# A float32 5x5 convolution layer, twice: banded 128x128 products against sixteen 32x32 tiles of the TensorE array

## Chip, cores and metric

One core of one Trainium2 chip. The metric is the device time of one execution in microseconds, the median of several runs. Everything is float32: the input, the weights, the products and the result.

## What is computed

Two layers of x = x + conv5x5(groupnorm(x)) on an array of 8 images, 32 channels, 252 x 252. Cut to what matters:

```python
def conv(x, weight):                       # reflect-padded by 2, circular, through the FFT
    xp = jnp.pad(x, ((0, 0), (0, 0), (p, p), (p, p)), mode='reflect')
    wp = jnp.roll(wp, shift=(-k // 2, -k // 2), axis=(-2, -1))      # -3: -5 // 2
    out = ifft2(einsum('bihw,oihw->bohw', fft2(xp), fft2(wp))).real
    return out[:, :, p:-p, p:-p]

def _gn(v, G=16, eps=1e-5):                # 16 groups of 2 channels over the whole image
    g = v.reshape(B_, G, C_ // G, H_, W_)
    m = jnp.mean(g, axis=(2, 3, 4), keepdims=True)
    s = jnp.var(g, axis=(2, 3, 4), keepdims=True)
    return ((g - m) / jnp.sqrt(s + eps)).reshape(v.shape)

x = x + conv(_gn(x), L0_conv_weight)
x = x + conv(_gn(x), L1_conv_weight)
```

Each output value is a sum over 32 input channels and 25 taps. Because of the roll, the rows and columns that a tap reads run from -1 to 254; -1, 252 and 253 are reflections, and 254 wraps to image row or column 2. The statistics of a layer need the whole image, so the second layer of an image can't begin before its first layer has ended.

## The kernel before

The 128 partitions are four quadrants of 32 channels. An image is cut into slots of four rows, one row per quadrant, so that a slot's result fills all 128 partitions of a PSUM tile. An output slot needs the padded rows of two neighbouring slots of the input, `blk` 0 and 1. For each of the 5 column taps there are therefore two products over the whole 128x128 array. Their weights `wt` (built once, lines 84 to 96) are banded: the 32x32 block for input row q and output row r is the tap a = r + 4 - 4 blk - q where that lies in 0 to 4, and zero elsewhere. Of the 2 x 4 x 4 = 32 blocks of a column tap, 4 x 5 = 20 hold weights, so 5/8 of the multiplications count.

An image is 8 chunks of 8 slots (the last has 7). `x` stays in SBUF from load to store, up to two images of it. `finish_stats` (lines 122 to 148) turns the collected moments into mean and 1/std: a VectorE aggregate, a one-column product `pm` that averages over a group's partitions, a few VectorE steps, a second one-column product `pv`, a square root on ScalarE, a Newton step on VectorE. `normalise` (from line 153) writes a chunk of `g`, the normalised, shifted and padded input: four VectorE operations (line 162) and four small ScalarE copies for the padding columns (lines 182 to 185). `conv` (from line 188) takes two slots at a time, 504 columns: 10 products into one PSUM bank (line 201), or 15 where the two slots straddle a chunk and each column range is cut in two halves of 252, then one VectorE addition of the residual into `x` (line 209).

The run (from line 212) goes image by image, layer by layer, chunk by chunk, and normalises one chunk ahead of the products; behind the last chunk of layer 1 the first chunk of the next image is normalised already. The moments for the next image (line 118) are taken during layer 0, those for layer 1 behind each residual addition. Loads and stores are on SyncE's queue; the loads of two images are issued at the start.

## Time and profile before

| what | value |
|---|---|
| median of 2 runs | 4437.72 us (4437.69 to 4437.75) |
| profiled execution, span from first to last instruction | 4439.0 us |
| TensorE (PE) busy | 4296.0 us, 97%, 11424 matmul records |
| weight loads (PEld) busy | 2159.0 us, 49%, as many records |
| VectorE (DVE) busy | 1375.4 us, 31% |
| ScalarE (ACT) busy | 103.1 us, 2% |
| GpSimd (POOL) busy | 7.3 us |
| moved by DMA | 132.59 MB, 30 GB/s over the span |

Times are microseconds from the start of the span, mean times of one instruction are nanoseconds. One float32 product of the program leaves two weight loads and two matmul records, called passes in the following: 5680 products of line 201, 11360 records. The end of a matmul record is modelled by the profiler, so the distance from one start to the next says more than its length. "Idle before" is the time in which the engine waited ahead of a group of instructions, with what ended the wait.

### The profile page before, as it was taken

How to read it: one execution, taken by the hardware profiler on the slowest of the kernel's cores; microseconds unless marked ns; L12 is line 12 of the kernel's file. 1: busy time of each engine (PE TensorE's matmuls, PEld its weight loads, DVE VectorE, ACT ScalarE, POOL GpSimd, SP SyncE). 2: the span in 40 equal slices, each digit the busy share in tenths (PEclk: the TensorE clock that was granted, in tenths of full speed). 3: DMA queues.
4: the chain of work that ended last, by engine and by line, in shares of the span. 5: the costliest groups of instructions: out<-in, count | busy, mean ns of one | idle time of the engine just before them, and what ended most of it. 6: DMA issues, size and time to landing. Idle time of an engine off the chain costs nothing.

```text
span 4439.0 us, 26427 instructions
## 1 busy us (share of the span) xinstructions
PE 4296.0 (97%) x11424; PEld 2159.0 (49%) x11424; DVE 1375.4 (31%) x1726; ACT 103.1 (2%) x609; POOL 7.3 (0%) x27
## 2 busy tenths in 40 slices
PE   4999999999999999999999999999999999999999
PEld 2454445444554445444544454454445544554444
DVE  6423332332333233332333323332322332232321
ACT  0000000000000000000000000000000000000000
POOL 0000000000000000000000000000000000000000
PEclk9999999999999999999999999999999999999999
DMA  9001320023100221002210023100320001100011
GB/s 173 0 0 38 65 44 1 0 47 64 36 0 0 56 55 36 0 0 56 55 36 1 0 56 65 27 0 0 66 55 8 0 10 28 28 9 1 10 28 36
DMA packets 137716, 132.59 MB, mean 30 GB/s; under 512 B 8320, under 2 KB 137344, under 8 KB 137600
## 3 DMA queue, kind: packets, MB, share of 16 engines
q1 hardware_dynamic: 137216, 130.09, 13.9%
q8 instruction: 89, 1.46, 0.1%
q10 hardware_dynamic: 384, 0.82, 0.1%
q14 instruction: 27, 0.22, 0.0%
HBM read 65.85 MB, written 65.03 MB: 29 GB/s over the span
## 4 chain that ended last, share of the span: by engine, by line
PE 97%; DVE 2%; DMA 1%; ACT 0%; issue 0%; SPq 0%; ACTq 0%; DVEq 0%
PE ps L201 96%; DVE g L162 1%; DMA x<-in_x_dram 1%; DVE mv L124 0%; PE pv L135 0%; DVE stats L118 0%; DMA wraw<-in_L_conv_weight_dram 0%; DVE x L209 0%; PE pm L127 0%; DVE dev L130 0%; DVE sq L133 0%; DVE sq L132 0%; ACT g L182 0%; DVE mr L128 0%; SPq L67 0%
## 5 line engine op out<-in xcount | busy, mean ns | idle before, releaser
L201 PE MATMUL ps<-g,wt 128*128 128x504 f32 (+1 forms) x11360 | 4282.6, 539 | 54.4 <-ACT g L185 54.4
L201 PEld LDWEIGHTS ps<-g,wt 128*128 128x128 f32 x11360 | 2147.7, 189 | 2186.5 <-issue 2076.2
L209 DVE TENSOR_TENSOR x<-ps,x 128x504 f32<-128x504 f32 (+1 forms) x512 | 345.1, 674 | 2435.6 <-PE ps L201 2432.5
L162 DVE TENSOR_SCALAR g<-x,mr 32x1764 f32<-32x1764 f32 (+4 forms) x496 | 668.7, 1365 | 578.1 <-PE ps L201 571.8
L118 DVE BATCH_NORM_STATS2 stats<-x 128x6 f32<-128x504 f32 (+1 forms) x512 | 325.2, 669 | 26.6 <-DMA x<-in_x_dram 18.7
L182 ACT COPY g<-g 128x8 f32<-128x8 f32 x128 | 26.2, 205 | 2766.5 <-DVE g L162 2734.5
L127 PE MATMUL pm<-mv,avg 128*128 128x1 f32 x32 | 6.4, 270 | 66.5 <-DVE mv L124 66.5
L127 PEld LDWEIGHTS pm<-mv,avg 128*128 128x128 f32 x32 | 5.3, 207 | 69.6 <-DVE mv L124 69.6
L184 ACT COPY g<-g 128x8 f32<-128x8 f32 x128 | 25.6, 200 | 0.0
L185 ACT COPY g<-g 128x8 f32<-128x8 f32 x128 | 25.6, 200 | 0.0
L183 ACT COPY g<-g 128x8 f32<-128x8 f32 x128 | 25.5, 199 | 0.2
L135 PE MATMUL pv<-sq,avg 128*128 128x1 f32 x32 | 8.0, 318 | 15.2 <-DVE sq L133 15.2
L140 ACT ACTIVATE std<-var 128x1 f32<-128x1 f32 x16 | 3.2, 203 | 800.2 <-DVE var L137 800.2
L181 ACT COPY g<-row 32x252 f32<-32x252 f32 x16 | 6.4, 399 | 432.9 <-PE ps L201 432.9
L124 DVE BATCH_NORM_AGGREGATE mv<-stats 128x2 f32<-128x192 f32 x16 | 15.4, 996 | 0.3
L135 PEld LDWEIGHTS pv<-sq,avg 128*128 128x128 f32 x32 | 6.6, 257 | 16.5 <-DVE sq L133 16.5
L174 ACT COPY g<-g 32x252 f32<-32x252 f32 x16 | 6.4, 401 | 204.2 <-DVE g L162 204.2
L179 ACT COPY g<-g 32x252 f32<-32x252 f32 x16 | 6.4, 401 | 28.3 <-DVE g L162 28.3
L180 ACT COPY g<-g 32x252 f32<-32x252 f32 x16 | 6.4, 400 | 0.2
L176 ACT COPY row<-g 32x252 f32<-32x252 f32 x16 | 6.4, 397 | 0.4
L95 DVE COPY wt<-wraw 32x160 f32<-32x160 f32 x20 | 4.9, 302 | 2.6 <-DMA wraw<-in_L_conv_weight_dram 2.6
L95 POOL COPY wt<-wraw 32x160 f32<-32x160 f32 x20 | 5.5, 315 | 5.5 <-DMA wraw<-in_L_conv_weight_dram 5.3
(21 smaller groups left out, 30.6 us busy)
## 6 DMA issues: line engine op xcount, KB each, us to landing
x<-in_x_dram SPq DMA_DIRECT2D x224, 252.0 KB, 5.2
out_dram<-x SPq DMA_DIRECT2D x224, 252.0 KB, 4.2
x<-in_x_dram SPq DMA_DIRECT2D x32, 220.5 KB, 4.6
out_dram<-x SPq DMA_DIRECT2D x32, 220.5 KB, 3.5
wraw<-in_L_conv_weight_dram ACTq DMA_DIRECT2D x8, 100.0 KB, 5.1
```

The lines of the kernel that those rows point to most:

```text
L95: eng.tensor_copy(t[quads[q], blk, :, (row + 1) % 4, :], wraw[l][quads[q], a, :, :])
L118: nc.vector.bn_stats(stats[b, l][:, (c * CH + j) // 2, :], xt[b, c][:, j : j + n, :].rearrange("p t w -> p (t w)"))
L124: nc.vector.bn_aggr(mv, stats.pop((b, l)).rearrange("p n s -> p (n s)"))
L127: nc.tensor.matmul(pm, avg, mv[:, 0:1], start=True, stop=True)
L135: nc.tensor.matmul(pv, avg, sq, start=True, stop=True)
L162: nc.vector.tensor_scalar(g[rows, dst, 1 : W + 1], src, mr[rows, 0:1], mr[rows, 1:2], ALU.subtract, ALU.mult)
L182: nc.scalar.copy(g[:, :, 0:1], g[:, :, 2:3])
L183: nc.scalar.copy(g[:, :, W + 1 : W + 2], g[:, :, W - 1 : W])
L184: nc.scalar.copy(g[:, :, W + 2 : W + 3], g[:, :, W - 2 : W - 1])
L185: nc.scalar.copy(g[:, :, W + 3 : W + 4], g[:, :, 3:4])
L201: nc.tensor.matmul(ps[:, at : at + m, :], wt[l][:, blk, kc, :], g[:, lo : lo + m, K - 1 - kc : K - 1 - kc + W], start=(i == 0), stop=(i == ...
L209: nc.vector.tensor_add(xs, ps[:, :n, :], xs)
```

## The change

The array is used as 16 tiles of 32x32: tile (g, m) takes its input from quadrant g of the partitions and writes quadrant m of a PSUM bank. All 25 taps of a 32x32 block are products of their own, accumulated in place; no block is zero.

Image layout. In `x0`, the input of layer 0, quadrant q holds rows 63q - 1 to 63q + 65 of the image, 256 columns wide: a row strip with its halo, so some rows are loaded twice. In `x1`, the input of layer 1, quadrant q holds a strip of 63 columns with its halo over all 256 padded rows. A layer takes 8 chunks of 8 rows (the last has 7); a product covers 8 rows x 63 columns, 504 columns, or 441 in the last chunk. The four banks `ps[g]` of a chunk are fed from the four input quadrants, and in each bank the four column tiles m hold the four pieces in the other direction, so that layer 0 turns row strips into column strips and layer 1 turns them back.

`products` issues, per chunk, 25 taps x 4 m x 4 g = 400 products with g innermost. `finish_stats` additionally builds the weights of this image and layer, `wt` = `wraw` / std + `center`, where `center` is the identity at the tap that reads the pixel itself, which is the residual. The mean goes into a bias: a third one-column product `pb` from `wsum`, a quarter of the sum of the raw weights over the taps in each quadrant. No normalised copy is made any more. Evacuation is four ScalarE activations per chunk that add the bias, into `x1` (with VectorE moments behind each) or into a result tile `y` that is stored. `halo`, `halo_rows` and `pad_cols` fill the padding by GpSimd copies. `x0` and `x1` are single buffers: a chunk of the next image is loaded when the products of layer 0 that read it are done. PSUM is one pool of eight banks, shared by the chunks and the small products.

```diff
-    ps_conv = ctx.enter_context(tc.tile_pool(name="ps_conv", bufs=6, space=bass.MemoryType.PSUM))
-    ps_stat = ctx.enter_context(tc.tile_pool(name="ps_stat", bufs=2, space=bass.MemoryType.PSUM))
+    psum = ctx.enter_context(tc.tile_pool(name="psum", bufs=8, space=bass.MemoryType.PSUM))
...
+    x0 = const.tile([P, S + 4, W + 4], F32, tag="x0", name="x0")
+    x1 = const.tile([P, H + 4, S + 4], F32, tag="x1", name="x1")
...
     def finish_stats(b: int, l: int):
...
         nc.vector.tensor_mul(mr[:, 1:2], inv, fix)
-        norm[b, l] = mr
...
+        wt = wpool.tile([P, K * K, C], F32, tag="wt", name=f"wt_{b}_{l}")
+        nc.vector.scalar_tensor_tensor(wt, wraw[l], mr[:, 1:2], center, ALU.mult, ALU.add)
+
+        rm = small.tile([P, 1], F32, tag="rm", name=f"rm_{b}_{l}")
+        nc.vector.scalar_tensor_tensor(rm, mr[:, 0:1], -1.0, mr[:, 1:2], ALU.mult, ALU.mult)
+        pb = psum.tile([P, 512], F32, tag="conv", name=f"pb_{b}_{l}")
+        nc.tensor.matmul(pb[:, 0:1], wsum[l].rearrange("p q o -> p (q o)"), rm, start=True, stop=True)
+        bias = small.tile([P, 1], F32, tag="bias", name=f"bias_{b}_{l}")
+        nc.vector.tensor_copy(bias, pb[:, 0:1])
+        return wt, bias
...
+    def products(b: int, l: int, k: int, wt):
+        n = rows[k]
+        ps = [psum.tile([P, 512], F32, tag="conv", name=f"ps_{b}_{l}_{k}_{g}") for g in range(4)]
+        for a in range(K):
+            for c in range(K):
+                t = a * K + c
+                for m in range(4):
+                    for g in range(4):
+                        if l == 0:
+                            r0, c0 = k * CH + 4 - a, S * m + 4 - c
+                            src = x0
+                        else:
+                            r0, c0 = S * m + k * CH + 4 - a, 4 - c
+                            src = x1
+                        nc.tensor.matmul(
+                            ps[g][quads[m], : n * S],
+                            wt[quads[g], t, :],
+                            src[quads[g], r0 : r0 + n, c0 : c0 + S],
+                            start=(t == 0),
+                            stop=(t == K * K - 1),
+                        )
+        return [p[:, : n * S].rearrange("p (n s) -> p n s", s=S) for p in ps]
+
+    def evac0(b: int, k: int, ps, bias):
...
+        for g in range(4):
+            dst = x1[:, S * g + k * CH + 1 : S * g + k * CH + 1 + n, 1 : S + 1]
+            nc.scalar.activation(dst, ps[g], AF.Identity, bias=bias)
+            nc.vector.bn_stats(st[:, k * 4 + g, :], dst)
...
+    for k in range(NCH + 1):
+        load(0, k)
...
     for b in range(B):
...
+        wt, bias = finish_stats(b, 0)
+        for k in range(NCH):
+            ps = products(b, 0, k, wt)
+            evac0(b, k, ps, bias)
+            halo(k)
+            if b + 1 < B and k:
+                load(b + 1, k - 1)
+        halo_rows()
...
+        wt, bias = finish_stats(b, 1)
+        for k in range(NCH):
+            if b + 1 < B:
+                stats0(b + 1, k)
+                pad_cols(k)
+            ps = products(b, 1, k, wt)
+            evac1(b, k, ps, bias)
```

How the order of TensorE's products moves, at the two places of which the prediction speaks. A name such as `ps_0_0_2_317` is a PSUM tile of layer 0, chunk 0, first slot 2 before the change, and of layer, chunk and input quadrant g after it; the last number is only a serial number. A row stands for one product of the program, or for as many as its "x" says.

The first products of an image on PE, before:

```order
L201 MATMUL ps_0_0_0_302<-g_0_0_280,wt_163 128x504 x10
L201 MATMUL ps_0_0_2_317<-g_0_0_280,wt_163 128x504 x10
L201 MATMUL ps_0_0_4_331<-g_0_0_280,wt_163 128x504 x10
L201 MATMUL ps_0_0_6_345<-g_0_0_280,wt_163 128x504 x5
```

and after:

```order
L190 MATMUL ps_0_0_0_256<-x_70,wt_0_248 32x504
L190 MATMUL ps_0_0_1_257<-x_70,wt_0_248 32x504
L190 MATMUL ps_0_0_2_258<-x_70,wt_0_248 32x504
L190 MATMUL ps_0_0_3_259<-x_70,wt_0_248 32x504
L190 MATMUL ps_0_0_0_256<-x_70,wt_0_248 32x504
L190 MATMUL ps_0_0_1_257<-x_70,wt_0_248 32x504
L190 MATMUL ps_0_0_2_258<-x_70,wt_0_248 32x504
L190 MATMUL ps_0_0_3_259<-x_70,wt_0_248 32x504
```

Before, ten products in a row fill one bank. After, each product names another input quadrant than the one ahead of it, and the same tile of the array comes back after 16 products, with the next tap.

Between layer 0 and layer 1 of an image on PE, before:

```order
L201 MATMUL ps_0_7_6_829<-g_0_7_713,wt_163 128x252 x10
L127 MATMUL pm_1_845<-mv_1_842,avg 128x1
L135 MATMUL pv_1_853<-sq_1_850,avg 128x1
L127 MATMUL pm_0_1380<-mv_0_1377,avg 128x1
L135 MATMUL pv_0_1388<-sq_0_1385,avg 128x1
L201 MATMUL ps_1_0_0_886<-g_1_0_866,wt_185 128x504 x10
```

and after, here and then between layer 1 of an image and layer 0 of the next:

```order
L190 MATMUL ps_0_7_3_3239<-x_70,wt_0_248 32x441
L142 MATMUL pm_1_3679<-mv_1_3676,avg 128x1
L150 MATMUL pv_1_3687<-sq_1_3684,avg 128x1
L170 MATMUL pb_1_3704<-rm_1_3702,wsum_83 128x1
L190 MATMUL ps_1_0_0_3717<-x_71,wt_1_3700 32x504
```

```order
L190 MATMUL ps_1_7_3_6667<-x_71,wt_1_3700 32x441
L142 MATMUL pm_0_7084<-mv_0_7081,avg 128x1
L150 MATMUL pv_0_7092<-sq_0_7089,avg 128x1
L170 MATMUL pb_0_7109<-rm_0_7107,wsum_77 128x1
L190 MATMUL ps_0_0_0_7113<-x_70,wt_0_7105 32x504
```

Before, the small products of the next image's layer 0 stand between layers 0 and 1 of this one, and nothing of the kind stands between images. After, `pm`, `pv` and `pb` stand ahead of the first product of each of the 16 layers.

## The prediction, made before the changed kernel had run

> **What bounds the kernel now.** I read the page's totals and its chain first, then the groups of line 201 with their shapes kept apart, then the timeline of weight loads in a quiet stretch.

> ```profile
> span 4439.0 us, 26427 instructions
> PE 4296.0 (97%) x11424; PEld 2159.0 (49%) x11424; DVE 1375.4 (31%) x1726; ACT 103.1 (2%) x609; POOL 7.3 (0%) x27
> PE 97%; DVE 2%; DMA 1%; ACT 0%; issue 0%; SPq 0%; ACTq 0%; DVEq 0%
> ```

> The chain that ended last runs through PE for 97%. What PE does there, and at which pace:

> ```profile
> L201 PE MATMUL ps<-g,wt 128*128 128x504 f32 x8800 | 3757.9, 586 | 54.4 <-ACT g L185 54.4
> L201 PE MATMUL ps<-g,wt 128*128 128x252 f32 x2560 | 564.9, 375 | 0.0
> L209 DVE TENSOR_TENSOR x<-ps,x 128x504 f32<-128x504 f32 x496 | 338.4, 682 | 2384.3 <-PE ps L201 2381.2
> L118 DVE BATCH_NORM_STATS2 stats<-x 128x6 f32<-128x504 f32 x496 | 319.2, 677 | 26.3 <-DMA x<-in_x_dram 18.7
> ```

> ```profile
> 1000.09 0.19 PEld L201 LDWEIGHTS ps<-g,wt 128*128 128x128 f32 x1 [0.23 <-issue]
> 1000.51 0.19 PEld L201 LDWEIGHTS ps<-g,wt 128*128 128x128 f32 x1 [0.23 <-issue]
> ...
> 1005.59 0.19 PEld L201 LDWEIGHTS ps<-g,wt 128*128 128x128 f32 x1 [0.24 <-issue]
> ```

> The mean of 586 ns is no price, since records overlap. The price is the distance of starts: 13 passes in 5.50 us, 0.423 us for a pass of 504 columns. A pass of 252 is taken at half, 0.2115. So 8800 x 0.423 + 2560 x 0.2115 = 4264 us, 96% of the span: the kernel is bound by columns streamed through the array. Weight loads fit into the shadow of the passes (0.19 of each 0.42 us), and VectorE waits for PE.

> **What the change removes.** Before, 158,760 columns per image and layer went through the whole array (63 slots x 252 x 10 products). After, each of 16 tiles has 25 taps x 63 x 63 = 99,225 columns, 5/8 of that. In passes: 8 images x 2 layers x 8 chunks x 400 = 51,200 products, 102,400 passes, 89,600 of 504 columns and 12,800 of 441 (0.370 us in proportion). If all 16 tiles stream side by side at the pace above: (89,600 x 0.423 + 12,800 x 0.370) / 16 = 2665 us.

> **What it adds: nine times as many loads and passes.** No row shows a 32x32 tile. The nearest rows are one-column products, where the load alone sets the pace:

> ```profile
> 879.18 0.19 PEld L135 LDWEIGHTS pv<-sq,avg 128*128 128x128 f32 x1 [1.19 <-DVE sq L133]
> ...
> 879.29 0.19 PEld L135 LDWEIGHTS pv<-sq,avg 128*128 128x128 f32 x1
> 879.39 0.19 PEld L127 LDWEIGHTS pm<-mv,avg 128*128 128x128 f32 x1
> ```

> ```profile
> 879.42 0.25 PE L127 MATMUL pm<-mv,avg 128*128 128x1 f32 x1
> ```

> Three loads start 0.105 us apart with a one-column pass between: that is a load of 128 columns plus a pass of nothing. A tile's load has 32 columns. If the time goes with columns, a load and its pass cost 0.026 us, and 102,400 of them, one at a time, 2688 us. If nothing shrinks, 0.105 us and 10,750 us. If loads into different tiles overlap, less than 2688, and the 2665 of the columns is the bound. I take 2688: the row is a load of the same engine and type, and I see no fixed part in it that I could separate. The two bounds lie within 1% of each other, so there is no slack: a fifth more per load gives 3226.

> The rest of the sum are stretches in which PE stands still. Today's, between layers 0 and 1 of image 1:

> ```profile
> 874.65 1.01 PE L201 MATMUL ps<-g,wt 128*128 128x252 f32 x4
> 877.69 0.38 PE L127 MATMUL pm<-mv,avg 128*128 128x1 f32 x2 [2.02 <-DVE mv L124]
> ...
> 881.32 0.15 DVE L147 TENSOR_TENSOR mr<-inv,fix 128x1 f32<-128x1 f32 x1
> ...
> 886.97 5.43 PE L201 MATMUL ps<-g,wt 128*128 128x504 f32 x8 [5.76 <-ACT g L185]
> ...
> 889.65 0.34 PEld L201 LDWEIGHTS ps<-g,wt 128*128 128x128 f32 x1 [0.50 <-issue]
> 890.49 0.25 PEld L201 LDWEIGHTS ps<-g,wt 128*128 128x128 f32 x1 [0.50 <-issue]
> 890.97 0.19 PEld L201 LDWEIGHTS ps<-g,wt 128*128 128x128 f32 x1 [0.24 <-issue]
> ```

> It is 11.3 us, 5.5 of them for normalising. From `pm` to 1/std takes 3.8 (877.69 to 881.47). Behind it the first four passes go at 0.84 instead of 0.42 us, at half the clock: 1.7 us lost. For the new operations I use

> ```profile
> L182 ACT COPY g<-g 128x8 f32<-128x8 f32 x128 | 26.2, 205 | 2766.5 <-DVE g L162 2734.5
> L174 ACT COPY g<-g 32x252 f32<-32x252 f32 x16 | 6.4, 401 | 204.2 <-DVE g L162 204.2
> L124 DVE BATCH_NORM_AGGREGATE mv<-stats 128x2 f32<-128x192 f32 x16 | 15.4, 996 | 0.3
> L95 POOL COPY wt<-wraw 32x160 f32<-32x160 f32 x20 | 5.5, 315 | 5.5 <-DMA wraw<-in_L_conv_weight_dram 5.3
> ```

> ScalarE: 0.196 us for 244 columns more, so 0.6 us for an evacuation of 504 and 0.55 for one of 441. VectorE: 682 ns for 504 elements with two inputs, so 1.1 us for the 800 weights.

> Layer 0 to layer 1, eight times: last evacuations 4 x 0.55 = 2.2, last moments 0.6, aggregate 1.0, `pm` to 1/std 3.8, weights 1.1, `pb` behind them 0.6 = 9.3 us, 74 in all. GpSimd's ten `halo` and four `halo_rows` copies at about 0.3 (4.2 us) start with the last evacuation and end under the VectorE chain; without that cover they would cost 4. Layer 1 to the next image's layer 0, seven times: today nothing, since the next image is normalised ahead. After, `pm`, `pv` and `pb` stand in PE's order behind the last product of the image, so 3.8 + 1.1 + 0.6 = 5.5 us lie open, 38 in all. Behind each of the 15 gaps 1.7 us for the half clock: 25.

> ```profile
> 53.71 1.33 DVE L162 TENSOR_SCALAR g<-x,mr 64x2016 f32<-64x2016 f32 x1
> ```

> ```profile
> 4432.54 2.61 SPq L72 DMA_DIRECT2D out_dram<-x  x4
> ```

> Head: the statistics of the first image are ready at 53.7 us; weights and `pb` add 1.7 and the extra halo rows under one: 56. Tail: today 6.5 us from the last store's issue to the end, plus four evacuations: 9.

> At nothing I cost the folded normalisation, the addition and the padding, as PE covers them: 768 moments x 0.68 = 520 us of VectorE, 512 evacuations x 0.6 = 310 of ScalarE, some 930 small GpSimd copies x 0.3 = 280, all spread under 2700 us. The loads of the next image wait for layer 0's products of the same rows and have all of layer 1 to land.

> **Sum:** 2688 + 56 + 74 + 38 + 25 + 9 = 2890 us, against the 4439.0 of the profiled execution, which lies 1.3 above the median; 2890 stands for both. What surrounds the products is 202 us. The break-even follows: 4439 - 202 = 4237 us for the products, which is 0.0414 us per pass, or 10.1 tiles busy on average out of 16.

> [...] No run here shows tiles yet; the forecast rests on passes that follow each other without draining, as the rows of 1000 us show for the whole array.

> **Rivals.** (a) *The two passes of one product stand in each other's way.* Every product is load, pass, load, pass on the same tile. In the rows at 1000 us the pace is that of one pass at a time. If TensorE starts passes strictly in order, the second pass waits 0.423 us for the first, everything behind it waits too, and only the second pass of one product and the first of the next overlap. Two tiles are busy: 2665 x 8 + 202 = 21,500 us. It decides as soon as fewer than 10.1 tiles stay busy. For it: the in-order pace of today's passes. Against it: they all use the whole array, so no row shows whether a free tile may start past a busy one. [...]

> (b) *A load and a pass have a price that doesn't shrink.* In the rows at 879 us a pass starts 0.03 us after its load (879.39, 879.42). If that is the time to issue an instruction and loads (0.026) and passes take turns, a pair costs some 0.052 us: 102,400 x 0.052 + 202 = 5530 us. It decides above 0.0414. For it: nothing in the trace hides instructions this small. Against it: a part of the 0.03 may be the load's own.

> (c) *Faster, but held back.* Fewer than 16 tiles busy on average, because tiles drain before they start anew (13 tiles give 3480 us, 10.3 give 4340), or PE waiting for its instructions:

> ```profile
> q8 instruction: 89, 1.46, 0.1%
> x<-in_x_dram SPq DMA_DIRECT2D x224, 252.0 KB, 5.2
> ```

> 22,848 loads and passes were fetched in 89 packets, so 204,800 need about 800, one every 3.4 us where it was one every 50. If each refill cost 5.2 us, as a transfer of `x` does from issue to landing, and nothing ran ahead, that is 4160 + 202 = 4360, hardly a gain; if they are read ahead, nothing. Between them, 3450 to 4350.

> **How the numbers follow.** Forecast: 0.48, own range 2840 (2665 for the products, gaps a little smaller) to 3450 (a fifth more per load, 3226 + 202). (c) 0.15. Within 2%, which is about what a measurement can tell from no change: 0.03. (b) 0.14, up to 6000. (a) 0.20. Faster 0.63, same 0.03, slower 0.34. From 2840 to 6000 lie 0.80; only (a) is left out.

> **What would show it.** Right: start to start of passes near 0.026 us, different tiles started before one has ended, PE's share of the chain above 90%, eight gaps of 9 us and seven of 5. (a) would show passes 0.42 us apart in pairs; (b) an even pace above 0.04 whatever the columns, so that the last chunks with 441 columns take as long as the others; (c) PE idle for "issue" at a regular distance of 256 instructions. The size of the gaps is wrong if `halo_rows` ends after the weights.

## The result

The changed kernel takes 3475.15 us (median of 2 runs, 3473.38 to 3476.93) against 4437.72 before: ratio 0.7831, 95% interval 0.7808 to 0.7853, so 22% faster. The forecast was faster, 2890 us. The direction and the surroundings of the products came out as worked out; the products themselves took 585 us more than the 2688 and the 25 for slow starts together.

The page of the kernel after, and two of its groups with shapes kept apart:

```profile
span 3475.2 us, 209222 instructions
PE 3305.6 (95%) x102496; PEld 2632.3 (76%) x102496; DVE 375.8 (11%) x755; ACT 307.6 (9%) x529; POOL 206.8 (6%) x971
...
q8 instruction: 802, 13.14, 1.6%
...
PE 90%; issue 6%; DVE 2%; DMA 1%; ACT 1%; ACTq 0%; DVEq 0%
```

```profile
L190 PE MATMUL ps<-x,wt 32*32 32x504 f32 x89600 | 2907.3, 601 | 14.3 <-issue 13.7
L190 PEld LDWEIGHTS ps<-x,wt 32*32 32x32 f32 x102400 | 2612.0, 103 | 682.4 <-issue 176.7
L190 PE MATMUL ps<-x,wt 32*32 32x441 f32 x12800 | 392.1, 542 | 8.5 <-issue 8.5
```

TensorE still carries the chain. The counts are those foretold, 89,600 and 12,800 passes, and 802 packets of instructions for the 800. The 95% of PE says nothing about full tiles, because a record of 601 ns counts as busy whether one tile or sixteen are at work. The distance of starts says it. The windows view of PE in an undisturbed stretch (length, busy time, passes in it, clock, share of DMA, GB/s):

```profile
1600.00:1700.00 100.00, 99.76 (x3154) 1.00 0.19 45
```

A pass every 0.0317 us, so 1.015 us for the 32 passes of 16 products, where the columns of 16 tiles take 0.846. Below I call these 16 products, one per tile, a turn. From the first to the last start of a layer's passes, summed over the 16 layers of the trace, the products take 3298 us; divided by 3200 turns that is 1.031, slow starts and the shorter turns of the last chunks included.

The rest of the span is 177 us: 52.9 ahead of the first product, eight gaps of 9.6 to 9.9 between layers 0 and 1, seven of 5.1 to 5.6 between images, 8.4 behind the last start. One gap of the first kind, from the timeline (start, length, engine):

```profile
258.48 3.33 PE L190 MATMUL ps<-x,wt 32*32 32x441 f32 x87
...
261.78 2.19 ACT L204 ACTIVATE x<-ps,bias 128x441 f32<-128x441 f32 x4 [23.19 <-PE ps L190]
...
264.66 1.02 DVE L139 BATCH_NORM_AGGREGATE mv<-stats 128x2 f32<-128x192 f32 x1
...
265.83 0.54 PE L142 MATMUL pm<-mv,avg 128*128 128x1 f32 x2 [4.02 <-DVE mv L139]
...
266.84 0.45 POOL L224 COPY x<-x 128x67 f32<-128x67 f32 x2
...
269.32 1.05 DVE L165 SCALAR_TENSOR_TENSOR wt<-wraw,mr,center 128x800 f32<-128x800 f32 x1
...
270.59 0.56 PE L170 MATMUL pb<-rm,wsum 128*128 128x1 f32 x2 [2.72 <-DVE rm L168]
271.08 0.28 PEld L190 LDWEIGHTS ps<-x,wt 32*32 32x32 f32 x32
```

Evacuations, moments, aggregate, `pm` to weights to `pb` follow each other as listed in the forecast, and the `halo_rows` copies (266.84) are done well before the weights.

The start of the first layer, same view, holds the key to the missing 585 us:

```profile
52.85 0.27 PEld L190 LDWEIGHTS ps<-x,wt 32*32 32x32 f32 x32
52.85 4.03 PE L190 MATMUL ps<-x,wt 32*32 32x504 f32 x64
...
53.69 0.17 PEld L190 LDWEIGHTS ps<-x,wt 32*32 32x32 f32 x1 [0.57 <-issue]
54.53 0.64 PEld L190 LDWEIGHTS ps<-x,wt 32*32 32x32 f32 x31 [0.67 <-issue]
55.37 0.17 PEld L190 LDWEIGHTS ps<-x,wt 32*32 32x32 f32 x1 [0.20 <-issue]
```

After a gap a pass takes 0.84 us, twice the 0.42 of the stream. Behind the next gap, where the starts have the same steps, the windows view (same columns) gives a granted clock of one half:

```profile
271.10:275.90 4.80, 4.80 (x93) 0.50 0.02 5
```

### The profile page after: what moved, and what is told of

The parts are those of the page before. It is cut to its first block, busy times and chain, and to the rows that moved or that the text cites. A ratio compares the mean times of both kernels' runs of the same rounds, so it can differ in the third digit from the quotient of the medians.

```text
span 3475.2 us, 209222 instructions
## 1 busy us (share of the span) xinstructions
PE 3305.6 (95%) x102496; PEld 2632.3 (76%) x102496; DVE 375.8 (11%) x755; ACT 307.6 (9%) x529; POOL 206.8 (6%) x971
## 3 DMA queue, kind: packets, MB, share of 16 engines
q8 instruction: 802, 13.14, 1.6%
## 4 chain that ended last, share of the span: by engine, by line
PE 90%; issue 6%; DVE 2%; DMA 1%; ACT 1%; ACTq 0%; DVEq 0%
PE ps L190 89%; DMA x<-in_x_dram 1%; ACT y L230 1%; DVE stats L205 1%; DVE wt L165 0%; DVE mv L139 0%; PE pb L170 0%; DMA wraw<-in_L_conv_weight_dram 0%; PE pv L150 0%; ACT x L204 0%; PE pm L142 0%; DVE fix L160 0%; DVE inv L157 0%; DVE mr L162 0%; DVE stats L135 0%
## 5 line engine op out<-in xcount | busy, mean ns | idle before, releaser
L190 PE MATMUL ps<-x,wt 32*32 32x504 f32 x102400 | 3284.0, 594 | 22.9 <-issue 22.2
L190 PEld LDWEIGHTS ps<-x,wt 32*32 32x32 f32 x102400 | 2612.0, 103 | 682.4 <-issue 176.7
L204 ACT ACTIVATE x<-ps,bias 128x504 f32<-128x504 f32 (+1 forms) x256 | 152.1, 679 | 1555.0 <-PE ps L190 1555.0
L230 ACT ACTIVATE y<-ps,bias 128x504 f32<-128x504 f32 (+1 forms) x256 | 151.8, 677 | 1525.4 <-issue 1233.8
L205 DVE BATCH_NORM_STATS2 stats<-x 128x6 f32<-128x504 f32 (+1 forms) x256 | 154.1, 665 | 1208.0 <-ACT x L204 1208.0
L215 POOL COPY x<-x 32x96 f32<-32x96 f32 x192 | 52.4, 273 | 2800.5 <-ACT x L204 2795.2
L135 DVE BATCH_NORM_STATS2 stats<-x 128x6 f32<-128x504 f32 (+1 forms) x256 | 154.0, 664 | 226.3 <-DMA x<-in_x_dram 226.2
L92 POOL COPY x<-x 128x8 f32<-128x8 f32 (+1 forms) x288 | 43.9, 201 | 232.9 <-DMA x<-in_x_dram 228.8
L170 PE MATMUL pb<-rm,wsum 128*128 128x1 f32 x32 | 8.7, 342 | 44.1 <-DVE rm L168 44.1
L216 POOL COPY x<-x 32x32 f32<-32x32 f32 x192 | 45.1, 235 | 8.6
L165 DVE SCALAR_TENSOR_TENSOR wt<-wraw,mr,center 128x800 f32<-128x800 f32 x16 | 16.8, 1052 | 0.6
L218 POOL COPY x<-x 32x32 f32<-32x32 f32 x64 | 15.4, 240 | 2.6
L219 POOL COPY x<-x 32x32 f32<-32x32 f32 x64 | 15.3, 239 | 0.0
L220 POOL COPY x<-x 32x32 f32<-32x32 f32 x64 | 15.1, 236 | 2.6
L217 POOL COPY x<-x 32x32 f32<-32x32 f32 x64 | 14.8, 232 | 2.7
## 6 DMA issues: line engine op xcount, KB each, us to landing
x<-in_x_dram SPq DMA_DIRECT2D x248, 252.0 KB, 4.9
out_dram<-y SPq DMA_DIRECT2D x224, 252.0 KB, 4.0
x<-in_x_dram SPq DMA_DIRECT2D x32, 31.5 KB, 2.7
```

The costliest lines, as they stand in the source:

```text
L92: nc.gpsimd.tensor_copy(x0[:, r, d : d + 1], x0[:, r, s : s + 1])
L135: nc.vector.bn_stats(st[:, (k * CH + i) // 2, :], x0[:, a : a + n, 1 : W + 1])
L165: nc.vector.scalar_tensor_tensor(wt, wraw[l], mr[:, 1:2], center, ALU.mult, ALU.add)
L170: nc.tensor.matmul(pb[:, 0:1], wsum[l].rearrange("p q o -> p (q o)"), rm, start=True, stop=True)
L190: nc.tensor.matmul(ps[g][quads[m], : n * S], wt[quads[g], t, :], src[quads[g], r0 : r0 + n, c0 : c0 + S], start=(t == 0), stop=(t == K * K ...
L204: nc.scalar.activation(dst, ps[g], AF.Identity, bias=bias)
```

## The experiments

The rivals of A: B, every load and pass has a fixed price of 0.0315 us; C, a tile's pass streams more slowly than one of the whole array; F, PE is paced by the fetching of its instructions. Times of single runs stand beside runs of the kernel before on the same chip, 4439 to 4441 us.

### Another order of the tiles

```diff
-                for m in range(4):
-                    for g in range(4):
+                for g in range(4):
+                    for m in range(4):
```

> Same products, but m innermost: four products in a row now share the input quadrant (row group) and differ in the column tile. The trace after shows 16 products taking 1.006 us on average where the columns alone would take 0.846, and 177 us around the products. Theory A (instructions are held only some 16 products ahead, so that a tile stands empty for 0.16 us between its products), theory B (every load and pass costs 0.0315 us, whatever its columns) and theory C (a pass of a tile streams more slowly than one of the whole array, 0.503 us for 504 columns) all expect the time after, 3475 within 1%. [...]

Measured: 3471.21 us, ratio to before 0.7818 (0.7805 to 0.7831); the interval overlaps that of the kernel after. Whether neighbouring products share an input quadrant makes no difference here.

### Unbroken rows of input

```diff
+                        flat = src.rearrange("p r w -> p (r w)")
...
-                            src[quads[g], r0 : r0 + n, c0 : c0 + S],
+                            flat[quads[g], r0 * src.shape[2] + c0 : r0 * src.shape[2] + c0 + n * S],
```

> Each product reads 504 (441) neighbouring columns in one run where it reads 8 (7) runs of 63: other data, so the output is not the reference's; all counts stay. Theory A and theory B: 3475, unchanged. Theory C, if the short runs are what slows a pass: 16 products in 0.846 us, 3200 x 0.846 + 71 of slow starts + 177 = about 2950.

Measured: 3461.56 us, one run, 14 less than the kernel after. So the short runs of 63 cost at most about that. C falls as far as it blamed them.

### Eight tiles in two quadrants

```diff
-        ps = [psum.tile(...) for g in range(4)]
+        ps = [psum.tile(...) for g in range(2)]
...
-                    for g in range(4):
+                    for g in range(2):
...
-        return [... for p in ps]
+        return [... for p in ps + ps]
```

> Half of the products are left out: only input quadrants 0 and 1, so 8 tiles; banks 2 and 3 are replaced by 0 and 1 in the evacuation. Theory A: 16 products held ahead are now two turns of each tile, so no tile waits, 8 products in 0.846 us, about 2950. Theory B: 8 products cost 0.503, less than the 0.846 that the columns take, so again about 2950. Theory C with a cause in each pass: 8 products in 1.006 us, 3475, unchanged; C with a shared limit (reads or writes of 16 streams): down towards 2950.

Measured: 5472.66 us, which no expectation had: half of the products, and longer than the kernel before. The groups and the timeline of that run:

```profile
L190 PE MATMUL ps<-x,wt 32*32 32x504 f32 x44800 | 4708.0, 1041 | 0.0
L190 PEld LDWEIGHTS ps<-x,wt 32*32 32x32 f32 x51200 | 1423.9, 171 | 3848.4 <-issue 3848.2
```

```profile
1600.08 0.22 PEld L190 LDWEIGHTS ps<-x,wt 32*32 32x32 f32 x8 [0.62 <-issue]
1600.92 0.22 PEld L190 LDWEIGHTS ps<-x,wt 32*32 32x32 f32 x8 [0.62 <-issue]
1601.76 0.22 PEld L190 LDWEIGHTS ps<-x,wt 32*32 32x32 f32 x8 [0.62 <-issue]
```

Four products every 0.84 us, so eight in 1.68: that is two passes of 0.84, the length that a pass has at half clock (the records are 1041 ns long, as in the first microseconds after a gap, 52.85 to 53.89). The weight loads are longer too, 0.17 us as at 53.69 above against 0.10 in the kernel after. The whole run went at the pace of the half clock. The clock column of the windows view shows 1.00 for it, but the trace of this run holds no clock event at all, where that of the kernel after holds 32, so the column says nothing here. At that pace the eight tiles run without any loss between their products, 1.68 of 1.68. So a tile does not stand empty as such. But the hand-over, 0.17 us, is short beside passes of 0.84, and the test of A had to be made again at full clock, below.

### Half the columns

```diff
-                            ps[g][quads[m], : n * S],
+                            ps[g][quads[m], : (n if t == 0 else n // 2) * S],
...
-                            src[quads[g], r0 : r0 + n, c0 : c0 + S],
+                            src[quads[g], r0 : r0 + (n if t == 0 else n // 2), c0 : c0 + S],
```

> 24 of the 25 taps cover only the first half of the columns (252 of 504): work left out, all counts stay. Theory A: 0.423 + 0.16 = 0.583 us for 16 products, about 2170. Theory B: unchanged, 3475. Theory C: in proportion, 0.503, about 1920.

Measured: 3291.38 us, between B (3475) and A (2170), near B. The weight loads in the timeline show that neither number describes it:

```profile
1600.06 1.45 PEld L190 LDWEIGHTS ps<-x,wt 32*32 32x32 f32 x60
1602.52 2.26 PEld L190 LDWEIGHTS ps<-x,wt 32*32 32x32 f32 x128 [1.01 <-issue]
1606.82 0.24 PEld L190 LDWEIGHTS ps<-x,wt 32*32 32x32 f32 x32 [2.04 <-issue]
```

128 loads with their 128 passes are four turns. The burst that begins at 1602.52 has its later turns at

```profile
1603.16 0.38 PEld L190 LDWEIGHTS ps<-x,wt 32*32 32x32 f32 x32
1603.80 0.38 PEld L190 LDWEIGHTS ps<-x,wt 32*32 32x32 f32 x32
1604.44 0.33 PEld L190 LDWEIGHTS ps<-x,wt 32*32 32x32 f32 x26
```

so a turn takes 0.64 us. Then PE idles for 1 to 2 us and waits for nothing that the profile shows. 256 instructions are one fetch of 16 KB: in the kernel after, 13.14 MB and 204,992 loads and passes came in 802 packets. Inside a burst the pace is that of A, 0.42 for the columns and a hand-over, though the hand-over is 0.22 and not the 0.16 expected; why it is longer stays open. B, which has 1.01 a turn whatever the columns, is refuted, and so is C in proportion, 0.50. Between bursts F decides, if the idle time comes from the fetch; the next run tries it with hardly any transfers.

### Half the columns, hardly any transfers

```diff
-        for q in range(4):
+        for q in range(4 if b == B - 1 else 0):
             nc.sync.dma_start(out[b, ...
...
-            if b + 1 < B and k:
-                load(b + 1, k - 1)
...
-        if b + 1 < B:
-            for k in range(NCH - 1, NCH + 1):
-                load(b + 1, k)
```

together with the edit for half the columns.

> 24 of 25 taps with half of the columns, and no loads and stores for most images, as in the two runs apart. With half the columns 16 products took 0.65 us in the median but 0.97 on average, with 716 stalls of over 1 us. Theory F for this kernel: the stalls are PE waiting for instructions; if data transfers slow the fetch, they shrink and the time falls from 3291 towards 3200 x 0.65 + 250 = 2330; if the fetch alone needs 3.4 to 3.7 us for 16 KB, it stays within 200 us of 3291. If the stalls came from waits for data or PSUM, they would stay with other lengths and no regular distance.

Measured: 3125.39 us, 166 less, within the 200 that F gives if the fetch alone is slow. The loads of that run:

```profile
1600.55 2.76 PEld L190 LDWEIGHTS ps<-x,wt 32*32 32x32 f32 x128 [1.18 <-issue]
1604.30 2.26 PEld L190 LDWEIGHTS ps<-x,wt 32*32 32x32 f32 x128 [0.99 <-issue]
1607.77 0.24 PEld L190 LDWEIGHTS ps<-x,wt 32*32 32x32 f32 x32 [1.21 <-issue]
```

The idle time comes after each 128 loads, to the instruction. The records of the instruction packets settle the cause. In this stretch one packet of 16 KB moves from 1601.68 to 1602.85 and the next from 1605.47 to 1606.39, and the bursts begin 1.45 and 1.38 us behind their ends. Over the whole run a burst begins 1.39 us (median; 1.24 to 1.59 for nine in ten) behind the end of a packet, and the next packet starts 1.14 us (median) behind the burst's start. So PE waits for its instructions here, and it is the round of one packet at a time that is long: 1.14, 1.39 and the 1.06 us or so in which a packet itself moves are 3.59.

The bursts begin 3.75 and 3.47 us apart; over the run the products take 2948 us for 800 fetches, 3.69 us each, and with transfers 3111, 3.89. So 16 KB of PE's instructions came every 3.5 to 3.9 us in these two runs. The kernel after uses one in 4 x 1.031 = 4.12 us: it lies just above that pace.

### The whole kernel, hardly any transfers

The same edit of loads and stores alone.

> The kernel after with all its instructions of TensorE, without the loads of images 1 to 7 (image 0 stays and is used again) and without the stores of images 0 to 6: nearly all DMA left is the fetching of instructions. Theory A: 16 products still take 1.03 us, total 3475 less at most 70 for the slow starts. Theory F (PE is paced by its instruction fetch, 16 KB or 256 instructions in 4.0 us, and data transfers slow the fetch): the fetch and with it the 16 products get faster, towards 0.87 us, about 3000.

Measured: 3416.04 us, 59 less; a turn still takes 1.011 us (3236 us of products). This is A's number and not F's 3000. Fetching that is delayed by transfers costs the kernel after at most 59 us.

### Twelve tiles

```diff
-                    for g in range(4):
+                    for g in range(3):
```

with three banks per chunk, and bank 0 evacuated in place of bank 3.

> A quarter of the products is left out: input quadrants 0 to 2 only, 12 tiles; bank 3 is replaced by bank 0 in the evacuation. Theory A: 16 products held ahead are more than one turn, so no tile waits: 12 products in 0.846 to 0.87 us, about 3000. If every tile stood empty for 0.16 to 0.18 us between its products whatever is held ahead: 3475. If the clock falls to half, as the pass lengths of the run with 8 tiles show for that run: 12 products in 1.69 us, about 5600.

Measured: 2934.66 us. The products take 2754 us, 0.861 per turn of 12 with slow starts, against 0.833 for the columns (2665 / 3200; 0.846 for those of 504): with twelve tiles, where 16 products are more than a turn, the hand-over has gone. A quarter less work for TensorE removes 16%; 12 full tiles get through 13.9 products per us, 16 with a hand-over through 15.5.

### Two taps in a row

```diff
-            for c in range(K):
-                t = a * K + c
-                for m in range(4):
-                    for g in range(4):
+            for m, g, c in [(m, g, c) for c2 in (0, 2, 4) for m in range(4) for g in range(4) for c in range(c2, min(c2 + 2, K))]:
+                        t = a * K + c
```

> Same products in another order: a tile gets two taps in a row (taps 0 and 1, 2 and 3, then 4 alone of each row of taps), so four passes of one tile follow each other where it was two. Theory A (TensorE holds only some 16 products, 64 loads and passes, ahead): 16 products now belong to 8 tiles, so a turn of pairs takes 2 x 0.846 x 16/8 = 3.4 us where two single turns took 2.06; products 3298 x 7.8 / 5.15 = 5000, total about 5170, more if the clock falls to half as it did with 8 tiles. If each tile had a queue of its own: unchanged, 3475. If passes started strictly in order, one per tile at a time: over 20000.

Measured: 5276.14 us, against A's 5170. Same products, same result, only the order of taps and tiles. A hundred microseconds in the middle of a layer:

```profile
1900.00:2000.00 100.00, 100.00 (x2087) 1.00 0.10 23
```

20.9 passes per us where the kernel after has 31.5; over all products it is 20.1 (102,400 in 5095 us) against 31.0. This is the sharpest test, and the start of the first layer shows why. First the loads of this run from the timeline, then PE's passes of products in the first 0.81 us, here and in the kernel after (the first clock event of both traces lies later, so the 1.00 of these two rows says nothing):

```profile
53.39 0.27 PEld L188 LDWEIGHTS ps<-x,wt 32*32 32x32 f32 x17
54.24 0.35 PEld L188 LDWEIGHTS ps<-x,wt 32*32 32x32 f32 x9 [0.57 <-issue]
```

```profile
53.39:54.20 0.81, 0.81 (x8) 1.00 0.00 0
```

```profile
52.85:53.66 0.81, 0.81 (x16) 1.00 0.00 0
```

64 instructions now cover eight tiles: 16 loads and 8 passes go out, and the 17th load is the 65th instruction, that of the ninth tile. Its pass, the 66th, starts only at 54.46, 0.03 us after the record of the very first pass ends (53.39 + 1.04). The other tiles stand empty although nothing of theirs is in use, so it is the count of instructions that holds them and not two loads per tile. A queue per tile (3475) is refuted, and so is a strict order with one pass per tile (over 20,000).

### Eight tiles in four quadrants

```diff
+                        if m >= 2 and t:
+                            continue
...
-                            stop=(t == K * K - 1),
+                            stop=(t == K * K - 1 or m >= 2),
```

> Eight tiles again, but spread over all four input quadrants: column tiles 2 and 3 get only the first of their 25 taps, work left out. Theory A: 16 products held ahead are two turns of 8 tiles, 0.846 us per turn, 3200 x 0.85 + 250 = 2970 if the clock is full. If the clock follows how much of the array works, as the half clock of the run with 8 tiles in two quadrants suggests: 1.69 us per turn, about 5500. If that half clock came from using two input quadrants alone: 2970.

Measured: 2923.76 us; the products take 2747 us, 0.858 per turn, at full clock (0.977 granted over the run). With two turns of eight tiles under way there is no hand-over beside the 0.833 to 0.846 of the columns, as A says. The half clock of the run with eight tiles in two quadrants is not a matter of their number alone. Whether it came with the two input quadrants is not shown, since this run also keeps one turn of all 16 tiles per chunk.

### The normalising work put back

The first attempt used four VectorE operations per chunk that depended on nothing but the raw weights.

> The kernel after plus, per chunk, four VectorE operations on 32 x 2016 elements into a scratch tile that nobody reads: about the VectorE work per chunk that the normalising took before (some 5 to 8 us per chunk of 26). If the folding gave nothing by itself because that work lies beside TensorE: 3475 within 1%. If VectorE were near the path behind the evacuations: 8 to 16 gaps longer by 5 us or more, 3520 to 3600.

Measured: 3917.55 us, but it tests nothing. The program's order put all these operations ahead of the first two layers, as the waits show (engine, line, what it waited for, total, times, longest):

```profile
PE pm L142 <- DVE mv L139: 499.4, 9, 352.7
```

One wait of 353 us between the layers of the first image, and 136 us ahead of the first product where it was 53; all other gaps are unchanged. The second attempt reads the image and its statistics, as normalising did:

```diff
+            if l == 0:
+                v = x0[quads[h], 1 + k * CH : 1 + k * CH + n, 1 : W + 1].rearrange("p n (g s) -> p g n s", g=4)
+            else:
+                v = x1[quads[h], 1 : H + 1, 1 : S + 1].rearrange("p (g s) w -> p g s w", g=4)[:, :, k * CH : k * CH + n, :]
+            nc.vector.tensor_scalar(scratch[quads[h], :, :n, :], v, mr[quads[h], 0:1], mr[quads[h], 1:2], ALU.subtract, ALU.mult)
```

> The kernel after plus the VectorE work of normalising, image by image and layer by layer: four operations of 32 x 2016 elements per chunk, which read the image and the layer's mean and 1/std, into a scratch tile that nobody reads. Unlike the run before, they can't be moved ahead of the first image; in VectorE's order all 32 of a layer stand at the layer's start, some 40 to 70 us of its 205. If the folding gave nothing by itself, since that work lies beside TensorE: 3475 within 1%. If it disturbs TensorE or the transfers of the next image: over 3510.

Measured: 3476.67 us.

```profile
L188 DVE TENSOR_SCALAR scratch<-x,mr 32x2016 f32<-32x2016 f32 (+1 forms) x512 | 668.7, 1306 | 16.0
```

669 us of VectorE work, as much as the normalising took before (668.7 in line 162), change the time by 2 us. So beside the stream of products the folding saves nothing. What it does save is normalising ahead of the first product between two layers, which stood in today's gap with 5.5 us of 11.3; the new gap spends 4 of them on evacuations and weights.

### The next image's statistics earlier

The chain up to the weights is issued ahead of the last chunk of layer 1; only `pb` and the bias stay between the images.

```diff
+            if b + 1 < B and k == NCH - 1:
+                early = finish_stats(b + 1, 0)
             ps = products(b, 1, k, wt)
```

> The statistics chain of the next image (pm, pv, weights) is issued ahead of the last chunk of layer 1, only pb and the bias stay between the images. Seven gaps of 5.4 us shrink to about 1, with about 2.5 us of waiting ahead of the last chunk for pv and for PSUM banks that come free later: 2 to 4 us won per image, also by the clock that stays up, 15 to 30 us in all, 3445 to 3460. If the gaps between images were not on the path: 3475.

Measured: 3456.12 us, ratio to before 0.7782 (0.7769 to 0.7795), the fastest version that does the whole work. The end of an image in its timeline:

```profile
475.48 5.64 PE L193 MATMUL ps<-x,wt 32*32 32x441 f32 x173
...
481.05 0.38 PE L173 MATMUL pb<-rm,wsum 128*128 128x1 f32 x2
481.36 0.15 PEld L193 LDWEIGHTS ps<-x,wt 32*32 32x32 f32 x6
```

The seven gaps shrink from 5.4 to 0.8 us, 32 us in all. The products' stretches grow by 12 in sum (3310.6 against 3298.4): ahead of each of the seven last chunks, where `pm` and `pv` now stand, the starts of two products lie 2.1 us apart.

## Why the prediction was right in direction and short in size

**What bounds the kernel.** Right: columns through the array, before and mostly after. The twelve and the eight tiles at full clock need 2754 and 2747 us for turns whose columns take 2665, slow starts included, so the price of the columns side by side holds within 3% for them. With all 16 tiles it isn't reached: 3298.

**The surroundings.** 56 + 74 + 38 + 9 = 177 us were foretold for head, gaps and tail, and 177 were measured: head 52.9, eight gaps of 9.7 (9.3), seven of 5.4 (5.5), tail 8.4 (9). The chain of small steps could be added up from rows of the trace before. The half clock behind each gap is seen too, in the 0.84 us between starts after 52.85, and the clock events of the trace give one half for 3.4 to 10.2 us at each of the 15 gaps; against the pace of the stretch behind them, the first twelve turns of the 16 layers take 27 us longer in sum (25).

**What was hidden.** Right: evacuations, moments and padding lie beside TensorE, and the normalising work, put back beside the products, changes the time by 2 us.

**The step that failed** is the term of the sum for the products: "a load and its pass cost 0.026 us, and 102,400 of them, one at a time, 2688 us". It measured 3298 with the slow starts, against 2688 + 25. The price per pass came out as 0.0322, but it is not a price per pass. With half the columns a turn runs in 0.64 us inside a burst, with twelve tiles all 24 passes nearly fit into the time of the columns, and with two taps in a row the same passes cost 0.050 each. What stands in its place is a limit on what TensorE has under way: 16 products, one turn, so that each turn ends in a hand-over of about 0.17 us. I had looked for the cost of a load and not asked how far ahead TensorE can see; in the trace before, where one pass fills the array, nothing shows it.

Without that limit 2890 would hardly have come out either, by an estimate from the runs with half the columns: 800 fetches of instructions every 3.69 us, the pace with hardly any transfers, make 2948 us of products, about 3125 in all, and at 3.89 about 3290. Rival (c) had this fetch, with 5.2 us for each as an upper bound; the pace measured with half the columns is 3.5 to 3.9.

**The rivals.** (a), two passes of one product blocking the rest, is refuted: 3475 and not 21,500, and even two taps in a row keep some eight tiles busy. (b), a price that does not shrink, is refuted by the pace inside the bursts of the run with half the columns. Its own sign is missing too: with hardly any transfers the turns of the last chunks, 441 columns, take 0.92 us and the others 1.01. (c) is what happened: 2665 x 16 / 3298 = 12.9 tiles busy on average, for the reason it named first, that tiles are empty before they start anew. 3475 lies 25 us beyond the range that I gave the forecast, 2840 to 3450, and inside that of (c), which had 0.15 against 0.48. That it comes so near the forecast's upper end is luck: that end stood for loads dearer by a fifth, and it was not the price of a load.

## What to carry to other kernels

When an array is split into tiles, count instructions under way and not only columns. Here 64 were under way, four per float32 product, so a tile whose next product stands 16 places later was empty before each return: 1.015 us a turn with 16 tiles, where 0.846 were due, and 0.861 with twelve. Issue products of different tiles next to each other; the order of the loops decided between 3475 and 5276 us. And work out the pace of instructions: with half the columns one fetch of 256 came every 3.69 to 3.89 us on average, and four turns of 0.64 us, 2.56 together, took as long.

## What the runs showed that I had not expected

- Eight tiles in two input quadrants keep TensorE at the pace of the half clock for a whole run of 5471 us, without a clock event that says so: pass records of 1041 ns and starts 0.84 us apart where 0.42 is due. Eight tiles spread over all four quadrants, with one turn of all 16 per chunk, run at full clock (0.977 granted, 0.858 us per turn), and so do twelve tiles in three quadrants (0.975, 0.861). What decides was not tried.
- With half the columns 16 KB of PE's instructions arrived every 3.69 us with hardly any transfers, every 3.89 with all of them; for 800 such packets that makes 2948 and 3111 us of products, close behind the 3298 of the kernel after.
- The 32 loads of 16 products go out in 0.27 us (row 52.85), and the median distance between neighbouring starts of passes is 0.017 us in the kernel after, so issuing as such is not the limit.
